# Linear attention in a two-layer decoder: the gated levels built each from the one below, and the low-rank gate product taken a round ahead

## The chip, the cores and the metric

The program runs on one core of one Trainium2 chip. A core has five engines that run side by side[...]: TensorE (PE, with its weight loads shown as PEld), VectorE (DVE), ScalarE (ACT), GpSimd (POOL) and SyncE (SP). The metric is the device time of one launch in microseconds. Three runs of the kernel before gave 1299.35, 1300.39 and 1302.56 us; the median is 1300.39.

## What is computed

The reference is a decoder of two layers over x (8 sequences of 256 tokens, width 256). Each layer has an attention, a cross-attention and a mixture of experts, and each of the six is followed by an added residual and a layer norm. The change touches the first of the six alone, the gated linear attention:

```python
q = heads(x @ Wq, DK) * scale            # 4 heads of 64
k = heads(x @ Wk, DK)
v = heads(x @ Wv, DV)                    # 4 heads of 128
gk = heads(log_sigmoid(x @ gk_w1 @ gk_w2 + gk_b2) / 16, DK)
def step(S, inp):
    S = S * exp(g_t)[..., None] + k_t[..., None] * v_t[..., None, :]
    o_t = einsum('bhk,bhkv->bhv', q_t, S)
g = x @ Wg
o = rms(o) * g_norm_w * silu(g)
x = layernorm(x + o @ Wo)
```

gk_w1 is 256x16 and gk_w2 is 16x256, so the gate comes from a product of low rank. The output at token t is a sum over s up to t of v_s, weighted by q_t, k_s and the product of the decays exp(g) of all tokens between s and t.

## The kernel before

The kernel has no recurrence. It splits the sum over pairs (s, t) by levels. At level w (1, 2, 4, ..., 128, the list WIDTHS) tokens are cut into blocks of 2w; s lies in the left half of a block, t in the right half. The decay between them is the product from the middle of the block to t, which is multiplied into q, times the product from s to the middle, which is multiplied into k. So each level has its own queries ql and keys kl, and a plain product of the two gives all its pairs. Channels lie on the 128 partitions (two groups j of 128 channels, two heads h in each), tokens along the free axis; a tile of one batch is 128 x 2 x 256.

The function gla holds the stage. Its work is a list called steps; in round b each step is called for batch b plus an offset, and the rounds run from -2 to 6, with a last part for batch 7 that is mixed with the start of the cross-attention. The order of the list is the order of work on TensorE, and the scheduler then places the instructions of the other engines. In the order of the list, with the offset:

- decays (+1): p_r, the product with w1 (L51, written through the helper mm); VectorE copies it to rt (L234); p_z, the product with w2, where rt carries a row of ones for the bias; ScalarE then takes Abs, Exp, Ln (L242 to L244), VectorE the difference e (L245), ScalarE the Exp that gives al (L246). Then the loop over levels: ql is qT times al on the right halves (L255, VectorE), kl is kT times be on the left halves (L260, POOL). tot (L267) holds the products of whole blocks; be (L271, POOL) and al (L275, VectorE) are multiplied by them on one half each to reach the next level. be is set to one and takes its first values on POOL (L250, L269).
- near (0), for chunk 0 and later for chunk 1 of 128 tokens: six small products p_near in 32x32 blocks, levels up to 16; a masked multiplication m (L310), a sum s (L315), and four copies into aT (L319), two of them on VectorE and two on POOL.
- turn (-1): transposes of the outputs of the batch before, pt_o (L374), copied to oT.
- far (0): the levels 32, 64 and, for chunk 1, 128: p_far, copied by ScalarE into aT and bT (L340 to L346).
- values and gates (+1): p_v and p_g; project (-1): p_y, residual and norm (L110 to L122).
- outputs (0): p_o from aT, bT and v; the square on ScalarE (L358), its sum ss on VectorE (L360), a power on POOL (L362), the scaled result on (L365).
- turn_in (+2): transposes of the input batch, pt_in, copied to xT (L209); turn_batch (-1): transposes of the normalised x, pt_x, copied to xT (L130).
- queries_keys (+2): p_q and p_k; qT is scaled by VectorE (L220), kT copied by ScalarE (L222).

ql and kl are kept in tiles that are set to zero once at the start, two for each level (L188), because each level writes only one half of each block and the other half has to stay zero. PSUM has one pool of eight banks that every product takes from in turn.

Of the kernel before, what the change touches and what calls it, by code (L numbers as in the profile page):

```python
# [10 lines left out]
F32 = mybir.dt.float32  # L11
BF16 = mybir.dt.bfloat16
I32 = mybir.dt.int32
AF = mybir.ActivationFunctionType
# [4 lines left out]
P = 128  # L19
# [20 lines left out]
def decoder_kernel(ctx: ExitStack, tc: tile.TileContext, a, out):  # L40
# [7 lines left out]
    def mm(dst, pairs):  # L48
        n = len(pairs)
        for i, (l, r) in enumerate(pairs):  # L50
            nc.tensor.matmul(dst, l, r, start=(i == 0), stop=(i == n - 1))  # L51
# [101 lines left out]
    def gla(late_loads):  # L153

        back = ExitStack()
        bw = back.enter_context(tc.tile_pool(name="gla_bw", bufs=1, side="right", reuse_waits="tile"))
        bk = back.enter_context(tc.tile_pool(name="gla_bk", bufs=2, side="right", reuse_waits="tile"))  # L160
# [2 lines left out]
        gp = front.enter_context(tc.tile_pool(name="gla_g", bufs=2, reuse_waits="tile"))  # L163
        wk = front.enter_context(tc.tile_pool(name="gla_wk", bufs=2, reuse_waits="tile"))

        w1 = load_k(wp, "w1", a["L0_attn_gk_w1"], 16, nc.scalar)
        w2 = wp.tile([17, 256], F32, tag="w2", name="w2")
        nc.scalar.dma_start(out=w2[0:16, :], in_=a["L0_attn_gk_w2"])
        nc.scalar.dma_start(out=w2[16:17, :], in_=a["L0_attn_gk_b2"].unsqueeze(0))
        gw = load_col(bw, "gw", a["L0_attn_g_norm_w"], nc.scalar)  # L170
        wq = load_k(wp, "wq", a["L0_attn_Wq"], 256)
        wkk = load_k(wp, "wkk", a["L0_attn_Wk"], 256)
# [18 lines left out]
            return r  # L191

        made = []
        rts = kept(wp, [17, S], "rt", 1.0)
        qls, kls = {w: [] for w in WIDTHS}, {w: [] for w in WIDTHS}
        for i in range(2):
            for w in WIDTHS:
                for n, l in (("q", qls), ("k", kls)):
                    if n == "q" or w > 1:
                        l[w] += kept(wp, [P, 2, S], f"{n}l{w}_{i}_", 0.0, 1)  # L200
        aTs = kept(bw, [P, 2, 2, P], "aT", 0.0, 4)
        qT, kT, v, gate, bT, po_, on, y = {}, {}, {}, {}, {}, {}, {}, {}

# [7 lines left out]
        def queries_keys(b):  # L211
            for name, w, d in (("q", wq, qT), ("k", wkk, kT)):
                d[b] = gp.tile([P, 2, S], F32, tag=name, name=name + "T")
                p = ps.tile([P, 2, S], F32, tag="ps", name="p_" + name)
                for j in range(2):
                    mm(p[:, j, :], [
                        (w[:, dc, j * P:(j + 1) * P], xT[:, dc, S * b:S * (b + 1)]) for dc in range(2)
                    ])
                if name == "q":
                    nc.vector.tensor_scalar(d[b], p, 0.125, None, ALU.mult)  # L220
                else:
                    nc.scalar.copy(  # L222
                        d[b].rearrange("p j t -> p (j t)"), p.rearrange("p j t -> p (j t)")
                    )

        def halves(t, w):

            return t.rearrange("p j t -> p (j t)").rearrange("p (n h w) -> p n h w", h=2, w=w)

        def decays(b):  # L230
            rt = rts[b % 2]
            p = ps.tile([P, 2, S], F32, tag="ps", name="p_r")
            mm(p[0:16, 0, :], [(w1[:, dc, :], xT[:, dc, S * b:S * (b + 1)]) for dc in range(2)])
            nc.vector.tensor_copy(rt[0:16, :], p[0:16, 0, :])  # L234
            z = ps.tile([P, 2, S], F32, tag="ps", name="p_z")
            for j in range(2):
                mm(z[:, j, :], [(w2[:, j * P:(j + 1) * P], rt)])

            e = wk.tile([P, 2, S], F32, tag="e", name="e", bufs=1)
            al = gp.tile([P, 2, S], F32, tag="al", name="al")  # L240
            flat = [t.rearrange("p j t -> p (j t)") for t in (e, z, al)]
            nc.scalar.activation(flat[0], flat[1], AF.Abs)  # L242
            nc.scalar.activation(flat[0], flat[0], AF.Exp, scale=-1.0)
            nc.scalar.activation(flat[0], flat[0], AF.Ln, bias=ones[:, 0:1])  # L244
            nc.vector.scalar_tensor_tensor(e, z, 0.0, e, ALU.min, ALU.subtract)  # L245
            nc.scalar.activation(flat[2], flat[0], AF.Exp, scale=1.0 / 16.0)  # L246


            be = gp.tile([P, 2, S], F32, tag="be", name="be")
            nc.gpsimd.memset(be, 1.0)  # L250
            tot = flat[2]
            for w in WIDTHS:
                n = 2 * S // (2 * w)
                pair = tot.rearrange("p (n h) -> p n h", h=2)
                nc.vector.tensor_tensor(  # L255
                    halves(qls[w][b % 2], w)[:, :, 1, :], halves(qT[b], w)[:, :, 1, :],
                    halves(al, w)[:, :, 1, :], ALU.mult,
                )
                if w > 1:
                    nc.gpsimd.tensor_tensor(  # L260
                        halves(kls[w][b % 2], w)[:, :, 0, :], halves(kT[b], w)[:, :, 0, :],
                        halves(be, w)[:, :, 0, :], ALU.mult,
                    )
                if w == WIDTHS[-1]:
                    break
                nxt = gp.tile([P, n], F32, tag=f"tot{w}", name=f"tot{w}")
                nc.vector.tensor_tensor(nxt, pair[:, :, 0], pair[:, :, 1], ALU.mult)  # L267
                if w == 1:
                    nc.gpsimd.tensor_copy(halves(be, 1)[:, :, 0, 0], pair[:, :, 1])  # L269
                else:  # L270
                    nc.gpsimd.tensor_tensor(  # L271
                        halves(be, w)[:, :, 0, :], halves(be, w)[:, :, 0, :],
                        pair[:, :, 1:2].broadcast_to([P, n, w]), ALU.mult,
                    )
                nc.vector.tensor_tensor(  # L275
                    halves(al, w)[:, :, 1, :], halves(al, w)[:, :, 1, :],
                    pair[:, :, 0:1].broadcast_to([P, n, w]), ALU.mult,
                )
                tot = nxt

        def values(b, c):
            if c == 0:
# [12 lines left out]
        def near(b, c):  # L295

            p = [ps.tile([P, 2, NEAR, 32], F32, tag="ps", name="p_near") for _ in range(2)]
            for l in range(NEAR):
                w = 2 ** l // 2
                k = kls[w][b % 2] if w > 1 else kT[b]  # L300
                q = qls[w][b % 2] if w else qT[b]
# [12 lines left out]
            for h in range(2):  # L314
                nc.vector.tensor_reduce(s[:, h], m[:, h].rearrange("p j l t -> p j t l"), AX.X, ALU.add)  # L315
            aT = aTs[2 * (b % 2) + c]
            for i in range(4):
                r = slice(32 * i, 32 * i + 32)
                (nc.gpsimd.tensor_copy if i % 2 else nc.vector.tensor_copy)(aT[r, :, :, r], s[r])  # L319

        def far(b, c):
# [3 lines left out]
            for w, s0, s1, t0, t1 in ((64, 0, 64, 64, 128), (32, 0, 64, 32, 64), (32, 64, 128, 96, 128)):  # L325
                for j in range(2):
                    for h in range(2):
                        r = slice(64 * h, 64 * h + 64)
                        mm(p[h][s0:s1, 0, j, t0:t1], [
                            (kls[w][b % 2][r, j, o + s0:o + s1], qls[w][b % 2][r, j, o + t0:o + t1])  # L330
                        ])
            if c:
                for j in range(2):
                    for h in range(2):
                        r = slice(64 * h, 64 * h + 64)
                        mm(p[h][:, 1, j, :], [(kls[P][b % 2][r, j, 0:P], qls[P][b % 2][r, j, P:S])])

            aT = aTs[2 * (b % 2) + c]
            for h in range(2):
# [38 lines left out]
        def project(b):  # L378
# [7 lines left out]
            (decays, 1),  # L386
            (near, 0, 0),
            (turn, -1, 0),
            (far, 0, 0),
            (values, 1, 0),  # L390
            (turn, -1, 1),
# [6 lines left out]
            (outputs, 0, 0),  # L398
            (turn_in, 2),
            (outputs, 0, 1),  # L400
            (turn_batch, -1),
            (queries_keys, 2),
        ]
        for b in range(-2, B - 1):
            run(round_of(steps, b))
# [987 lines left out]
```

## Time and profile before

| what | value |
|---|---|
| median of three runs | 1300.39 us |
| the profiled run | 1301.57 us |
| its span, first to last instruction | 1299.8 us |
| mean granted clock of TensorE | 0.888 |
| busy: PE, PEld, DVE, ACT, POOL | 1054.2, 692.1, 655.3, 448.4, 339.9 us |
| DMA, mean rate over the span | 48 GB/s |

The linear attention takes about the first 300 us of the span. The page's second part gives the busy share of each engine in tenths, in 40 slices of 32.5 us; the first nine slices are this stage:

```
PE   6888888888898649999997468888998888873870
DVE  6667676654555432222222544444444566764325
ACT  3445454424444212212121134333443444330104
POOL 7545555430111021111111730000000110101544
```

A line of a timeline has the start, the length, the engine, the line of the code, the operation, and what it writes and reads; the brackets at its end give the time that the engine sat idle before it, and what released it. A chain of waits is followed back from the last instruction of a window: at each step to what released it, or to the instruction before it on its engine. In a table of groups, the numbers at the end are the busy time of the group, the mean length of one in ns, and the idle time before them.

### The profile page before, as it was taken

To read this page: it belongs to the slowest core of one execution; us is meant where nothing else is said; L and a number is where in the kernel's file an instruction comes from. 1 tells how busy PE (TensorE), PEld (TensorE's weight loads), DVE (VectorE), ACT (ScalarE), POOL (GpSimd) and SP (SyncE) were. 2 spreads that over 40 slices of the span, in tenths; PEclk is the share of its full clock that TensorE was granted. 3 is DMA by queue.
4 is the path that set the end of the run, shared out by engine and by line. 5 is a ranking of instruction groups with operands and counts; after the bars stand their busy time and mean duration, and the time that the engine had idled before them with its cause. 6 is when DMAs were issued, how large, how long until landed. Compare 5 with 4: busy or idle time off the path is not lost.

```text
span 1299.8 us, 25292 instructions
## 1 busy us (share of the span) xinstructions
PE 1054.2 (81%) x10221; PEld 692.1 (53%) x10221; DVE 655.3 (50%) x1833; ACT 448.4 (34%) x874; POOL 339.9 (26%) x454
## 2 busy tenths in 40 slices
PE   6888888888898649999997468888998888873870
PEld 4556665665665426666665235555555555652540
DVE  6667676654555432222222544444444566764325
ACT  3445454424444212212121134333443444330104
POOL 7545555430111021111111730000000110101544
PEclk9789988889999659999999689899999998975895
DMA  7000000003111291111111210000000010105425
GB/s 191 3 2 2 3 3 2 2 3 130 34 33 34 61 303 45 49 41 49 45 45 57 77 49 2 1 1 1 2 1 1 2 33 18 34 24 150 138 82 174
DMA packets 54517, 62.64 MB, mean 48 GB/s; under 512 B 10897, under 2 KB 45858, under 8 KB 54402
## 3 DMA queue, kind: packets, MB, share of 16 engines
q1 hardware_dynamic: 46368, 44.59, 10.6%
q0 software_dynamic: 5616, 15.34, 4.2%
q8 instruction: 82, 1.34, 0.4%
q10 hardware_dynamic: 2418, 1.09, 0.4%
q14 instruction: 33, 0.27, 0.1%
HBM read 42.78 MB, written 18.22 MB: 47 GB/s over the span
## 4 chain that ended last, share of the span: by engine, by line
PE 56%; DVE 24%; ACT 5%; POOL 5%; issue 4%; DMA 4%; SPq 0%; POOLq 0%; ACTq 0%; DVEq 0%
PE p_y L51 6%; PE p_u L1013 5%; PE p_y L1035 5%; PE p_v L1013 5%; PE p_pv L51 4%; DVE m L687 3%; PE p_q L51 3%; PE p_v L51 3%; PE p_s L681 3%; PE p_st L585 2%; PE p_k L51 2%; PE p_st L696 2%; DVE tot L267 2%; DVE al L275 2%; PE p_s L51 2%
## 5 line engine op out<-in xcount | busy, mean ns | idle before, releaser
L687 DVE TENSOR_REDUCE m<-p_s 128x2 f32<-128x512 f32 x128 | 80.1, 683 | 31.8 <-PE p_s L681 31.8
L1019 DVE TENSOR_TENSOR h<-h,p_v 128x512 f32<-128x512 f32 x39 | 26.8, 688 | 121.1 <-PE p_v L1013 121.1
L896 POOL DMA_INDIRECT xg<-rows,tok x39 | 37.0, 949 | 178.3 <-PE pt_g L1002 158.9
L122 DVE TENSOR_TENSOR y<-p_y,xb 128x512 f32<-128x512 f32 x24 | 16.5, 688 | 118.0 <-PE p_y L51 118.0
L1013 PE MATMUL p_u<-fw,xgT 128*128 x156 | 75.3, 606 | 0.6 <-DVE xgT L1004 0.6
L499 POOL TENSOR_TENSOR xb<-x,L_xattnbo 128x512 f32<-128x512 f32 x16 | 20.3, 1271 | 210.6 <-DVE y L122 169.6
L703 ACT ACTIVATE e<-p_st 128x512 f32<-128x512 f32 x128 | 66.9, 643 | 22.6 <-PE p_st L468 20.2
L1035 PE MATMUL p_y<-fw,hT 128*128 x312 | 73.8, 379 | 0.7 <-ACT hT L1028 0.7
L1013 PE MATMUL p_v<-fw,xgT 128*128 x156 | 74.0, 597 | 0.0
L1035 PEld LDWEIGHTS p_y<-fw,hT 128*128 128x128 f32 x312 | 59.2, 190 | 25.2 <-issue 18.2
L592 ACT ACTIVATE e<-p_st 77x512 f32<-77x512 f32 x128 | 65.7, 600 | 17.7 <-PE p_st L468 17.7
L1028 ACT COPY hT<-pt_h 128x512 f32<-128x512 f32 x39 | 22.8, 585 | 128.7 <-PE pt_h L1026 128.7
L477 ACT COPY u<-p_pv 128x512 f32<-128x512 f32 x48 | 28.1, 585 | 110.9 <-PE p_pv L51 109.9
L51 PE MATMUL p_pv<-e,vals 77*32 77x256 f32 (+1 forms) x1024 | 64.8, 394 | 0.0
L130 ACT COPY xT<-pt_x 128x512 f32<-128x512 f32 x40 | 23.4, 585 | 111.1 <-PE pt_x L129 110.5
L499 POOL TENSOR_TENSOR xb<-x,L_attnbo 128x512 f32<-128x512 f32 x8 | 10.1, 1268 | 189.4 <-DVE y L122 189.4
L129 PE MATMUL pt_x<-ident,x 128*128 128x128 f32 x160 | 28.2, 301 | 37.9 <-DVE x L115 37.5
L576 DVE TENSOR_REDUCE m<-p_s 128x4 f32<-128x308 f32 x128 | 53.0, 467 | 6.9 <-PE p_s L51 6.9
L51 PEld LDWEIGHTS p_pv<-e,vals 77*32 77x32 f32 (+1 forms) x1024 | 33.5, 112 | 32.0 <-issue 18.2
L1013 PEld LDWEIGHTS p_v<-fw,xgT 128*128 128x128 f32 x156 | 30.1, 193 | 38.2 <-issue 38.2
L681 PE MATMUL p_s<-kT,qT 32*128 32x512 f32 x256 | 50.0, 696 | 0.0
L260 POOL TENSOR_TENSOR kl<-kT,be 128x256 f32<-128x256 f32 x56 | 48.2, 861 | 4.4
(271 smaller groups left out, 2420.1 us busy)
## 6 DMA issues: line engine op xcount, KB each, us to landing
fw<-in_L_ffn_W SPq DMA_DIRECT2D x24, 512.0 KB
rows<-x SPq DMA_DIRECT2D x32, 256.0 KB
ys<-yo SPq DMA_DIRECT2D x39, 128.0 KB
m<-in_L_ffn_w SPq DMA_DIRECT2D x16, 256.0 KB
z<-ys SPq DMA_DIRECT2D x8, 512.0 KB
x<-in_x SPq DMA_DIRECT2D x8, 256.0 KB
out<-x SPq DMA_DIRECT2D x8, 256.0 KB
b<-in_L_ffn_b ACTq DMA_DIRECT2D x8, 128.0 KB
```

Source lines behind the costliest of these rows:

```text
L51: nc.tensor.matmul(dst, l, r, start=(i == 0), stop=(i == n - 1))
L129: nc.tensor.transpose(pt[:, dc, c, :], x[:, 2 * b + c, dc * P:(dc + 1) * P], ident)
L260: nc.gpsimd.tensor_tensor(halves(kls[w][b % 2], w)[:, :, 0, :], halves(kT[b], w)[:, :, 0, :], halves(be, w)[:, :, 0, :], ALU.mult,)
L499: nc.gpsimd.tensor_tensor(xb, x[:, 2 * b:2 * b + 2, :], self.bo.unsqueeze(1).broadcast_to([P, 2, D]), ALU.add)
L576: nc.vector.tensor_reduce(st.less(b)[:, c, j, :], p, AX.X, ALU.max, negate=True)
L592: nc.scalar.activation(e[0:KV].rearrange("p i q -> p (i q)"), p[0:KV].rearrange("p i q -> p (i q)"), AF.Exp)
L681: nc.tensor.matmul(tiles[j].rearrange("p a m -> p (a m)"), st.qT[b][r, t, c * P:(c + 1) * P], kTs[b][r, t, :, :].rearrange("p a m -> p (a ...
L687: nc.vector.tensor_reduce(st.less(b)[:, c, j, 2 * t:2 * t + 2], p, AX.X, ALU.max, negate=True)
L703: nc.scalar.activation(e.rearrange("p i q -> p (i q)"), p.rearrange("p i q -> p (i q)"), AF.Exp)
L896: nc.gpsimd.indirect_dma_start(out=out, out_offset=None, in_=table, in_offset=bass.IndirectOffsetOnAxis(ap=index, axis=0),)
L1013: nc.tensor.matmul(p, xg[:, dc, :], w[:, bass.ds(e * (2 * FF) + dc * FF, FF)], start=(dc == 0), stop=(dc == 1),)
L1035: nc.tensor.matmul(y, hT[:, f * P:(f + 1) * P], w3[:, bass.ds(e * (4 * D) + f * D, D)], start=(f == 0), stop=(f == 3),)
```

## The change

Six things are done.

1. levels is a step of its own, at offset +1, and stands behind near and turn of chunk 0 and ahead of far; decays ends with the logarithm.
2. The queries of a level are made whole, 512 columns, from the queries of the level below, and the keys from the keys below (`qls[w, b], q = t, t`). The multiplier is broadcast from a small tile halves[w] of 4 columns per block of 2w: one, the decay of the left half, that of the right half, one. The queries take columns 0 and 1 (left halves unchanged, right halves times the left one's decay), the keys columns 2 and 3. The other half of a block is no longer zero; near masks it, and far reads only the halves that it needs. al and be are gone, and so are the zeroed tiles of ql and kl; the new tiles rotate in the pool. The last level makes only the 128 columns that far reads.
3. The product of low rank is a step of its own, low_rank at +2, a round ahead of decays. Its two halves of the contraction are not accumulated but go to two column tiles of 32, and the sum is taken in p_z, with w2 stacked twice. The row of ones for the bias comes from an activation with a bias column, on ScalarE.
4. qT is scaled by ScalarE.
5. queries_keys and low_rank stand ahead of turn_batch.
6. At the start ScalarE's queue has seven loads, where it had five, and three small tiles of weights are set to zero on VectorE.

```diff
-        w1 = load_k(wp, "w1", a["L0_attn_gk_w1"], 16, nc.scalar)
-        w2 = wp.tile([17, 256], F32, tag="w2", name="w2")
+        w1 = wp.tile([P, 2, 32], F32, tag="w1", name="w1")
+        w2 = wp.tile([64, 256], F32, tag="w2", name="w2")
+        one = wp.tile([64, 1], F32, tag="one", name="one")
...
+        for i in range(2):
+            nc.scalar.dma_start(out=w2[32 * i:32 * i + 16, :], in_=a["L0_attn_gk_w2"])
         nc.scalar.dma_start(out=w2[16:17, :], in_=a["L0_attn_gk_b2"].unsqueeze(0))
+        nc.scalar.dma_start(out=one[16:17, :], in_=a["c_iota"][0:1, 1:2])
...
+        halves = {w: kept(wp, [P, S // w, 4], f"halves{w}", 1.0) for w in WIDTHS[:-1]}
...
-                if name == "q":
-                    nc.vector.tensor_scalar(d[b], p, 0.125, None, ALU.mult)
+                nc.scalar.activation(
+                    d[b].rearrange("p j t -> p (j t)"), p.rearrange("p j t -> p (j t)"),
+                    AF.Copy, scale=0.125 if name == "q" else 1.0,
+                )
+
+        def low_rank(b):
+            p = ps.tile([P, 2, S], F32, tag="ps", name="p_r")
+            for dc in range(2):
+                mm(p[32 * dc:32 * dc + 32, 0, :], [(w1[:, dc, :], xT[:, dc, S * b:S * (b + 1)])])
+            rts[b] = wk.tile([64, S], F32, tag="rt", name="rt")
+            nc.scalar.activation(rts[b], p[0:64, 0, :], AF.Identity, bias=one[:, 0:1])
...
+        def levels(b):
+            e, z = ez.pop(b)
+            two = [halves[w][b % 2][:, :, 1:3] for w in WIDTHS[:-1]]
             nc.vector.scalar_tensor_tensor(e, z, 0.0, e, ALU.min, ALU.subtract)
+            nc.scalar.activation(
+                two[0], e.rearrange("p j t -> p (j t)").rearrange("p (n h) -> p n h", h=2), AF.Exp, scale=1.0 / 16.0
+            )
+            q, k = qT[b], kT[b]
+            for l, w in enumerate(WIDTHS):
+                last = w == WIDTHS[-1]
+                if 0 < l < len(two):
+                    nc.vector.tensor_tensor(
+                        two[l], *(two[l - 1][:, :, h].rearrange("p (n i) -> p n i", i=2) for h in range(2)),
+                        ALU.mult,
                     )
+                for n, old, side in (("q", q, 1), ("k", k, 0)):
+                    if w == 1 and n == "k":
+                        continue
+                    t = gp.tile([P, 2, P if last else S], F32, tag=f"{n}l{w}", name=f"{n}l{w}")
...
+                        f = halves[w // 2][b % 2][:, :, 0:2] if n == "q" else halves[w // 2][b % 2][:, :, 2:4]
+                        if last:
+                            v[1], f = v[1][:, side::2], f[:, side::2]
+                        (nc.vector if n == "q" else nc.gpsimd).tensor_tensor(
+                            v[0], v[1], f.unsqueeze(3).broadcast_to(v[0].shape), ALU.mult
+                        )
...
             (decays, 1),
             (near, 0, 0),
             (turn, -1, 0),
+            (levels, 1),
             (far, 0, 0),
...
             (outputs, 0, 1),
+            (low_rank, 2),
+            (queries_keys, 2),
             (turn_batch, -1),
-            (queries_keys, 2),
         ]
```

More of the change, by code (lines that the diff above doesn't have):

```diff
@@ L164, in gla @@
         wk = front.enter_context(tc.tile_pool(name="gla_wk", bufs=2, reuse_waits="tile"))
-        w1 = load_k(wp, "w1", a["L0_attn_gk_w1"], 16, nc.scalar)
-        w2 = wp.tile([17, 256], F32, tag="w2", name="w2")
-        nc.scalar.dma_start(out=w2[0:16, :], in_=a["L0_attn_gk_w2"])
+        w1 = wp.tile([P, 2, 32], F32, tag="w1", name="w1")
+        w2 = wp.tile([64, 256], F32, tag="w2", name="w2")
+        one = wp.tile([64, 1], F32, tag="one", name="one")
+        nc.vector.memset(w1, 0.0)
+        nc.vector.memset(w2, 0.0)
+        nc.vector.memset(one, 0.0)
+        nc.scalar.dma_start(
+            out=w1[:, :, 0:16], in_=a["L0_attn_gk_w1"].rearrange("(c p) n -> p c n", p=P)
+        )
+        for i in range(2):
+            nc.scalar.dma_start(out=w2[32 * i:32 * i + 16, :], in_=a["L0_attn_gk_w2"])
         nc.scalar.dma_start(out=w2[16:17, :], in_=a["L0_attn_gk_b2"].unsqueeze(0))
+        nc.scalar.dma_start(out=one[16:17, :], in_=a["c_iota"][0:1, 1:2])
         gw = load_col(bw, "gw", a["L0_attn_g_norm_w"], nc.scalar)
@@ L193, in gla @@
         made = []
[L194 to L200, printed above, removed]
+        halves = {w: kept(wp, [P, S // w, 4], f"halves{w}", 1.0) for w in WIDTHS[:-1]}
+        qls, kls, rts, ez = {}, {}, {}, {}
         aTs = kept(bw, [P, 2, 2, P], "aT", 0.0, 4)
@@ L218, in queries_keys @@
                     ])
-                if name == "q":
[L220 to L228, printed above, removed]
+                nc.scalar.activation(
[8 more added lines that the diff above has]
+            nc.scalar.activation(rts[b], p[0:64, 0, :], AF.Identity, bias=one[:, 0:1])
         def decays(b):
[L231 to L234, printed above, removed]
+            rt = rts.pop(b)
             z = ps.tile([P, 2, S], F32, tag="ps", name="p_z")
@@ L239, in decays @@
             e = wk.tile([P, 2, S], F32, tag="e", name="e", bufs=1)
-            al = gp.tile([P, 2, S], F32, tag="al", name="al")
-            flat = [t.rearrange("p j t -> p (j t)") for t in (e, z, al)]
+            flat = [t.rearrange("p j t -> p (j t)") for t in (e, z)]
             nc.scalar.activation(flat[0], flat[1], AF.Abs)
@@ L244, in decays @@
             nc.scalar.activation(flat[0], flat[0], AF.Ln, bias=ones[:, 0:1])
+            ez[b] = e, z
+        def levels(b):
+            e, z = ez.pop(b)
+            two = [halves[w][b % 2][:, :, 1:3] for w in WIDTHS[:-1]]
             nc.vector.scalar_tensor_tensor(e, z, 0.0, e, ALU.min, ALU.subtract)
[L246 to L262, printed above, removed]
-                    )
[L264 to L279, printed above, removed]
@@ new lines, in levels @@
+            nc.scalar.activation(
[8 more added lines that the diff above has]
+                        ALU.mult,
+                    )
+                for n, old, side in (("q", q, 1), ("k", k, 0)):
+                    if w == 1 and n == "k":
+                        continue
+                    t = gp.tile([P, 2, P if last else S], F32, tag=f"{n}l{w}", name=f"{n}l{w}")
+                    if w == 1:
+                        nc.vector.tensor_tensor(
+                            t.rearrange("p j t -> p (j t)").rearrange("p (n h) -> p n h", h=2),
+                            old.rearrange("p j t -> p (j t)").rearrange("p (n h) -> p n h", h=2), two[0], ALU.mult,
+                        )
+                    else:
+                        v = [
+                            e.rearrange("p j t -> p (j t)").rearrange("p (n h w) -> p n h w", h=2, w=w // 2)
+                            for e in (t, old)
+                        ]
+                        f = halves[w // 2][b % 2][:, :, 0:2] if n == "q" else halves[w // 2][b % 2][:, :, 2:4]
[3 more added lines that the diff above has]
+                            v[0], v[1], f.unsqueeze(3).broadcast_to(v[0].shape), ALU.mult
+                        )
+                    if n == "q":
+                        qls[w, b], q = t, t
+                    else:
+                        kls[w, b], k = t, t
@@ L299, in near @@
                 w = 2 ** l // 2
-                k = kls[w][b % 2] if w > 1 else kT[b]
-                q = qls[w][b % 2] if w else qT[b]
+                k = kls[w, b] if w > 1 else kT[b]
+                q = qls[w, b] if w else qT[b]
                 for j in range(2):
@@ L329, in far @@
                         mm(p[h][s0:s1, 0, j, t0:t1], [
-                            (kls[w][b % 2][r, j, o + s0:o + s1], qls[w][b % 2][r, j, o + t0:o + t1])
+                            (kls[w, b][r, j, o + s0:o + s1], qls[w, b][r, j, o + t0:o + t1])
                         ])
@@ L335, in far @@
                         r = slice(64 * h, 64 * h + 64)
-                        mm(p[h][:, 1, j, :], [(kls[P][b % 2][r, j, 0:P], qls[P][b % 2][r, j, P:S])])
+                        mm(p[h][:, 1, j, :], [(kls[P, b][r, j, :], qls[P, b][r, j, :])])
             aT = aTs[2 * (b % 2) + c]
```

## The prediction

> **What bounds the kernel now.** I read the clock of the core first (one core, mean 0.888), then the slices of the page (TensorE busy in 8 or 9 tenths up to 300 us, so the linear attention is the stage to ask about), then the chain of waits inside it, then the timeline engine by engine. The change touches only this stage. One round of it, from one decay product p_z to the next, shown by the chain from 168 to 205 us (start, length, what):
>
> ```profile
> 169.60 0.60 DVE qT L220
> 170.20 0.33 DVE rt L234
> ...
> 170.57 1.14 PE p_z L51 x4
> ...
> 178.15 0.64 ACT al L246
> ...
> 193.04 0.43 DVE ql L255
> ...
> 196.30 0.42 DVE x L115
> ...
> 202.16 1.13 DVE on L365 x4
> 203.29 0.60 DVE qT L220
> 203.88 0.33 DVE rt L234
> ```
>
> The loop is closed through VectorE. The gates of the next batch need p_z, p_z needs rt, rt is copied by VectorE, and VectorE reaches that copy only behind the levels, the norm and the two output chunks. From the list: p_z to the end of al 8.2 us (170.57 to 178.79), levels and near work 14.7 (to 193.47), norm 3.6 (to 197.0), two chunks of outputs with their waits for POOL's power 6.3 (to 203.3), qT and rt 0.9. Sum 33.7, the distance to p_z at 204.26. TensorE, in its timeline, waits for exactly this:
>
> ```profile
> 196.86 0.67 PE L129 MATMUL pt_x<-ident,x 128*128 128x128 f32 x4 [0.81 <-DVE x L115]
> ...
> 204.26 1.12 PE L51 MATMUL p_z<-rt,w 17*128 17x256 f32 x4 [2.30 <-DVE rt L234]
> ```
>
> At the start the same wait is larger, because rt of batch 1 stands behind all levels of batch 0:
>
> ```profile
> 35.58 2.04 PE L51 MATMUL p_z<-rt,w 17*128 17x256 f32 x4 [6.68 <-DVE rt L234]
> ```
>
> p_z starts at 13.87, 35.58, 67.62, 103.28, 136.93, 170.57, 204.26, 238.74; the last pt_x is at 265.16. So rounds last 32.0, 35.7, 33.65, 33.64, 33.69, 34.5, and the last 26.4 to pt_x.
>
> **What leaves, comes and moves.** *VectorE gives up qT and rt* (0.60 + 0.33 us per round, on the loop); ScalarE takes both, 0.6 and about 0.45 (nearest row: L446, 128x256 from PSUM, 0.47), ahead of the kT copy, where it idled 2.9 us waiting for p_k. rt is now made a round ahead, so p_z waits only for its turn on TensorE.
>
> *TensorE's order.* p_r, p_q, p_k now stand before pt_x. p_r in two column tiles instead of one accumulated pair: 0.95 before, bounds 0.5 (the tiles run together) and 0.95; I take 0.55, at most 0.4 a round. pt_x comes some 4 us later against p_o; its result is read only by the stage after, so that costs nothing, but p_z now stands behind it and behind x. p_z has the same columns and costs the same.
>
> *Levels.* Before, per batch: 8 ql, 7 al, 7 tot on VectorE; a memset, a copy, 7 kl, 6 be on POOL. After: 7 ql of 512 columns, one of 256, 6 tot; 6 kl of 512, one of 256. In elements nothing is saved: VectorE 15x256 plus 508 against 7x512+256 plus 504, POOL's products 13x256 = 3,328 against 6x512+256 = 3,328. That matters because the two engines take turns. POOL's timeline and then VectorE's at the same moment:
>
> ```profile
> 189.02 0.89 POOL L271 TENSOR_TENSOR be<-be,tot 128x256 f32<-128x256 f32 x1
> 189.99 0.73 POOL L260 TENSOR_TENSOR kl<-kT,be 128x256 f32<-128x256 f32 x1
> ```
> ```profile
> 189.02 0.41 DVE L255 TENSOR_TENSOR ql<-qT,al 128x256 f32<-128x256 f32 x1
> ...
> 190.08 0.92 DVE L275 TENSOR_TENSOR al<-al,tot 128x256 f32<-128x256 f32 x1
> ```
>
> be, starting with ql, is longer than the 0.68 it takes elsewhere; al, starting inside kl, takes 0.92 instead of 0.41 and ends 0.28 after kl does: its own pass began when POOL let go. So halving the count saves only fixed parts. Prices of POOL's products:
>
> ```profile
> L260 POOL TENSOR_TENSOR kl<-kT,be 128x256 f32<-128x256 f32 x56 | 48.2, 861 | 4.4
> ...
> L271 POOL TENSOR_TENSOR be<-be,tot 128x256 f32<-128x256 f32 x48 | 37.0, 772 | 3.8
> ```
> ```profile
> L499 POOL TENSOR_TENSOR xb<-x,L_xattnbo 128x512 f32<-128x512 f32 x2 | 2.5, 1264 | 0.1
> ```
>
> The trace has no wide kl, so bounds: 1.27 (the wide xb, 1.271 over the page, also with one operand broadcast, VectorE idle) and 1.72 (twice the 0.861). I take 1.27 and add VectorE's turns separately. The Trainium skill, "GPSIMD Engine Reference", section "Performance versus the Vector engine", speaks against leaving these on POOL: about 2.6 cycles per element for two inputs. On top of the 0.861 that makes 0.861 + 256 x 2.6 / 1.2 GHz = 1.42 each, an estimate, 0.9 us more per round than 1.27. The row has the same shape and decides; the 0.9 stays in the range.
>
> POOL from al to the last half of aT was 15.16 us (178.79 to 193.95). After: 6 x 1.27 + 0.86 = 8.5, gaps 0.6. VectorE's own passes there are about 4,344 elements at 1.0 ns ((688 - 433) / 256, rows L1019 and L255) = 4.3; 7 gaps and dispatches take in some 1.4 of them, so POOL is stretched by 2.9. Then VectorE's reduction for the second chunk must end and POOL copies aT (0.83): about 1.5 more. The sum is 13.5; in a second count over VectorE (passes 4.7, tots 1.25, m and s 2.4, waits for POOL 5.5 of its 7.5 us, then aT) it is 14.8. I take 14.3. If VectorE waited only as long as before (4.1) it would be 12.9, if for all 7.5, 16.3.
>
> *POOL's order.* Its aT copies of chunk 0 (1.17 us, amid the levels before) now stand ahead of the first kl; they wait for s, which is done 3 us before the Exp, so they cost nothing unless near is late.
>
> *The exponential comes later.* In the changed kernel's order ScalarE does six copies from p_far (1.25 us) before the Exp with its table load (1.93), and VectorE two m and two s (2.5) before e. From the end of p_z: near 3.2, m and s to 5.7, e 6.4; the far copies to 7.0; Exp to 9.0. Before it was 7.1 (171.7 to 178.79).
>
> **The new loop.** End of p_z to Exp 9.0; to aT of chunk 1, 14.3; p_o of chunk 1 behind it 1.8; p_r 0.55, p_q 1.73, p_k 1.77, pt_x 0.55 (durations start to start); p_z 1.05; handovers 0.5. That is 31.3 us against 33.65. What is late next is POOL's chain and aT, not rt. VectorE's output chunks end about 2 us into the next round, where near still runs: covered; if not, m starts that much later.
>
> **The start.** The 30 zeroed 128x512 tiles of ql and kl go (VectorE 7.3 us, POOL 7.2), replaced by small ones: worth nothing, since VectorE's first qT at 11.66 waited only on p_q, and POOL was idle from 11.6. ScalarE issues seven loads instead of five; the sixth waits for the slot of the first batch's load (landed 3.9), so the table load ends near 6.2 and xT comes at 6.8 instead of 5.64; with p_q and p_k at half rate and p_r in front, the first Exp is 0.9 late. Then VectorE: levels of batch 0 11.5 from 21.8, four casts 2.4, near work and e 3.2, Exp 1.95 = 40.9, where al began its levels at 45.0 before; 14.8, 1.8, 4.05 more bring the third p_z to 61.6, against 67.62: 6.0 gained. SP's and POOL's load queues keep their order; only slots shift.
>
> **Sum.** Start 6.0. Five rounds: before 171.1, after 5 x 31.3 plus 2 for the two rounds stretched by fetch stalls in near (2.5 and 2.15 us of "issue") = 158.5: 12.6 gained. The last round has no p_r, p_q, p_k to hide behind: 9.0 + 13.9 + norm 3.4 + handovers against 25.3 puts pt_x 1.4 later. Total 17.2. 1301.57 - 17.2 = 1284.4; the profiled run is 1.2 above the median of 1300.39, so **1283**. Nothing after 300 us changes but its start.
>
> **The clock.** The windows (start:end, length, TensorE, ...; the clock is third from the end):
>
> ```profile
> 172.00:174.00 2.00, 2.00 (x162) 1.94 (x161) 0.27 (x1) 1.97 (x3) 0.00 (x0) 0.55 0.04 8
> ...
> 180.00:182.00 2.00, 2.00 (x195) 1.83 (x193) 2.00 (x5) 0.98 (x2) 1.84 (x3) 1.00 0.03 8
> ```
>
> After the 2.3 us wait and the thin near products TensorE runs at half clock for 3 to 7 us in nearly every round: p_v at 176.79 takes 3.08 instead of 1.98. The Trainium skill, "TensorE: Matmul & The Clock Gate", section "HAM oscillation", asks for no idle gap over about 3.4 us; by that rule no gap here ever closes the gate and closing the wait wins nothing more. By the rows it closed after 2.3. I counted half of the slow time away (near 3.2, not 3.7); if all goes, near and far are 1.2 us shorter, 6 us over five rounds.
>
> **Rivals.** *TensorE becomes the bound* (0.15): if the turns cost less than before, only its own work is left: 26.5 us of products at full clock, 1.5 of fetch stalls, 1 of slow clock = 29.0 per round; 171.1 - 145 + 6 = 32, so 1268. For it: TensorE's waits are 3.4 us of 33.7. Against: the shared turns. *Only the start counts* (0.2): the later Exp and 16.3 for the levels give 33.3 per round; start 6, last round -1.4: about 1295. For it: element counts do not fall. *Slower* (0.06): the wide kl on POOL. Seven products now hang on one another, and every 0.1 us more of each of six costs 4.8 us over eight batches; from 1.27 + 17.2 / 48 = 1.63 us on, all is lost. At 1.8 (twice 0.86 to 0.99) it is 25.4 - 17.2 = 8 slower, 1308. Against: the 1.27 row. *It does not do what it says* (0.04): p_z held by another wait, no change, 1300.
>
> **Chances.** The forecast (0.55) spans 1275 to 1291. With the rivals, and 1272 to 1299 from the two bounds of the levels, I range from 1269 to 1297. 0.3% is 3.9 us, about what a measurement here can tell from no change. Faster 0.86 (forecast, TensorE, most of start-only), same 0.08, slower 0.06.
>
> **What would show it.** p_z no longer released by rt but following pt_x; the second p_z near 29 us; rounds of 31 to 32; wide kl at 1.3 to 1.6; p_o waiting for POOL's aT; Exp some 9 us behind p_z. Rounds of 29 with TensorE without waits would show the first rival, kl over 1.63 the slow one; a third p_z not before 65 us would break my start.

## The result, and the profile after

The changed kernel takes 1280.25 us (median of four runs, 1276.43 to 1281.39) against 1299.89 us before (a fourth run gave 1299.40): ratio 0.9839, 95% interval 0.982 to 0.9858, or 1.6% less. Timed again on another chip, where the kernel before took 1298.25, it was 0.9868 (0.9838 to 0.9898). The profiled execution took 1279.57 us, with a span of 1277.8 and a mean clock of 0.902; before, the span was 1299.8.

The predicted 1283 us lies close by. The parts of the prediction are another matter, and they begin with the chain of waits of the changed kernel over the round that answers to the one shown of before (start, length, what):

```profile
158.00 1.07 PE p_z L51 x4
...
166.58 0.69 ACT halves L257
...
167.99 1.64 DVE halves L264
...
179.74 0.72 DVE s L328
180.46 0.33 DVE ql L286
180.79 0.72 DVE s L328
...
181.96 0.30 POOL aT L332
182.26 0.04 issue
182.31 3.45 PE p_o L51 x16
185.75 0.56 PE p_r L51 x4
...
190.40 1.06 PE p_z L51 x4
```

rt has gone from the chain: behind p_k comes pt_x, then p_z at once. The chain now runs through the exponential (it ends at 167.27, 8.2 us behind the end of p_z and 9.3 behind its start), the levels, POOL's copy into aT (182.26, 15.0 later), and the second output chunk. TensorE's timeline at the same places, and at the second p_z of the kernel (start, length, engine, line, what, and in brackets the wait before it):

```profile
27.73 1.13 PE L51 MATMUL p_z<-rt,w 64*128 64x256 f32 x4
...
182.31 0.80 PE L51 MATMUL p_o<-v,aT 128*128 128x128 f32 x2 [2.66 <-POOL aT L332]
...
190.33 1.13 PE L51 MATMUL p_z<-rt,w 64*128 64x256 f32 x4
```

The second p_z starts at 27.73 without a wait, where it stood at 35.58 with 6.68 us of one. The new wait is 2.66 us for aT, and it is not all that it costs. The windows around it (the clock is the third number from the end):

```profile
178.00:180.00 2.00, 1.64 (x13) 1.25 (x11) 2.00 (x5) 1.36 (x3) 0.61 (x1) 1.00 0.00 0
180.00:182.00 2.00, 0.00 (x0) 0.00 (x0) 1.95 (x5) 0.31 (x1) 0.32 (x2) 0.96 0.00 0
182.00:184.00 2.00, 1.70 (x8) 1.70 (x9) 1.66 (x6) 0.00 (x0) 0.36 (x2) 0.50 0.00 0
184.00:186.00 2.00, 2.00 (x14) 1.71 (x13) 1.05 (x3) 0.21 (x1) 0.83 (x2) 0.68 0.00 0
186.00:188.00 2.00, 2.00 (x12) 1.58 (x9) 0.59 (x3) 0.82 (x2) 1.20 (x2) 1.00 0.00 0
```

In this round the half clock stands behind p_o's wait, where before it stood in the near products behind p_z's: the 16 products take 3.45 us. Not every round is like it. TensorE's lines of two other rounds, and one of e2, a run described below:

```profile
86.52 0.49 PE L51 MATMUL p_o<-v,aT 128*128 128x128 f32 x2 [0.77 <-POOL aT L332]
...
148.48 0.80 PE L51 MATMUL p_o<-v,aT 128*128 128x128 f32 x2 [2.84 <-POOL aT L332]
```
```profile
164.95 0.49 PE L51 MATMUL p_o<-v,aT 128*128 128x128 f32 x2 [2.94 <-POOL aT L322]
```

From p_z to this product it is 24.4 us in four of the five rounds that follow the third p_z, and 24.8 in the last. Behind waits of 0.77, 0.64 and 0.51 us the clock stayed full, and the next p_z followed 6.6 us later; behind 2.84 and 2.66 us it followed 9.4 and 8.0 us later. So the five rounds last 31.0, 31.0, 33.8, 32.4 and 31.4 us. The length of the wait alone does not settle the clock: in e2 it stayed at 1.00 behind 2.94 us. Over the five rounds the mean clock is 0.95, and was 0.91 before.

The levels, in the groups of the page (x48: six in each of eight batches; busy us, mean ns | idle time before, and its releaser):

```profile
L286 POOL TENSOR_TENSOR kl<-kl,halves 128x512 f32<-128x512 f32 (+1 forms) x48 | 60.0, 1249 | 20.6 <-DVE halves L264 18.9
...
L264 DVE TENSOR_TENSOR halves<-halves 128x256 f32<-128x256 f32 (+5 forms) x48 | 53.8, 1120 | 0.0
```

A total of 256 down to 8 columns takes 1.12 us on the mean. Why is seen where POOL's timeline is laid beside VectorE's:

```profile
169.80 1.57 POOL L286 TENSOR_TENSOR kl<-kl,halves 128x512 f32<-128x512 f32 x1 [0.67 <-DVE halves L264]
171.79 1.45 POOL L286 TENSOR_TENSOR kl<-kl,halves 128x512 f32<-128x512 f32 x1 [0.42 <-DVE halves L264]
...
176.72 1.06 POOL L286 TENSOR_TENSOR kl<-kl,halves 128x512 f32<-128x512 f32 x1 [0.19 <-DVE halves L264]
```
```profile
169.56 0.68 DVE L286 TENSOR_TENSOR ql<-ql,halves 128x512 f32<-128x512 f32 x1
170.16 1.46 DVE L264 TENSOR_TENSOR halves<-halves 128x128 f32<-128x128 f32 x1
```

The total begins at 170.16, while POOL is in kl, and ends at 171.62, 0.25 after kl does; the next kl then needs that total. In turn kl, begun inside ql, takes 1.57, and 1.06 where only the masking product m, which reads PSUM, was running when it began. The Trainium skill, "SBUF — State Buffer", section "SBUF: two separate sides", states the rule behind this: a GpSimd operation and a VectorE one with two SBUF inputs shut each other out for a whole instruction. Row and rule agree.

**Where the 22.0 us of the profiled execution come from.** The third p_z comes 5.5 us sooner (62.13 for 67.62); the five rounds to the eighth (221.77 for 238.74) give 11.5; the last round takes 1.1 back (pt_x of the sixth batch at 249.33 for 265.16). That is 15.8. Another 2.9 come up to the next pt_x, where batch 7 is mixed with the cross-attention: p_k and p_y, which took 2.72 and 5.69 us before (mean clock 0.66 from 276 to 286 us), take 1.50 and 3.72 (clock 1.00 from 261 to 268 us). Some 3.1 come in the last experts' stage, whose code is the same, from the first weight load to the first result fetched (77.6 before, 74.5 after). The run on the other chip had its eighth p_z at 220.41 and 74.3 for that stage.

### The profile page after: what moved, and what is told of

Its sections match the earlier page's. It is cut to its first block, busy times and chain, and to the rows that moved or that the text cites. A ratio compares the mean times of both kernels' runs of the same rounds, so it can differ in the third digit from the quotient of the medians.

```text
span 1277.8 us, 25121 instructions
## 1 busy us (share of the span) xinstructions
PE 1040.9 (81%) x10221; PEld 685.3 (54%) x10221; DVE 651.4 (51%) x1747; ACT 457.9 (36%) x890; POOL 308.8 (24%) x381
## 4 chain that ended last, share of the span: by engine, by line
PE 59%; DVE 22%; ACT 6%; POOL 4%; issue 4%; DMA 3%; SPq 1%; POOLq 0%; ACTq 0%; DVEq 0%
PE p_u L1028 5%; PE p_y L51 5%; PE p_y L1050 5%; PE p_v L1028 5%; PE p_pv L51 4%; PE p_q L51 3%; DVE halves L264 3%; DVE m L702 3%; PE p_k L51 3%; PE p_s L696 3%; DVE ql L286 3%; PE p_st L711 2%; PE p_v L51 2%; PE p_st L600 2%; PE p_s L51 2%
## 5 line engine op out<-in xcount | busy, mean ns | idle before, releaser
L702 DVE TENSOR_REDUCE m<-p_s 128x2 f32<-128x512 f32 x128 | 80.1, 684 | 32.1 <-PE p_s L696 32.1
L607 ACT ACTIVATE e<-p_st 77x512 f32<-77x512 f32 x128 | 65.8, 602 | 18.2 <-PE p_st L483 18.2
L286 POOL TENSOR_TENSOR kl<-kl,halves 128x512 f32<-128x512 f32 (+1 forms) x48 | 60.0, 1249 | 20.6 <-DVE halves L264 18.9
L130 ACT COPY xT<-pt_x 128x512 f32<-128x512 f32 x40 | 23.4, 585 | 107.7 <-PE pt_x L129 107.1
L264 DVE TENSOR_TENSOR halves<-halves 128x256 f32<-128x256 f32 (+5 forms) x48 | 53.8, 1120 | 0.0
L51 PEld LDWEIGHTS p_pv<-e,vals 77*32 77x32 f32 (+1 forms) x1024 | 33.7, 113 | 32.4 <-issue 18.4
```

What stands on the lines that cost most here:

```text
L264: nc.vector.tensor_tensor(two[l], *(two[l - 1][:, :, h].rearrange("p (n i) -> p n i", i=2) for h in range(2)), ALU.mult,)
L286: (nc.vector if n == "q" else nc.gpsimd).tensor_tensor(v[0], v[1], f.unsqueeze(3).broadcast_to(v[0].shape), ALU.mult)
L607: nc.scalar.activation(e[0:KV].rearrange("p i q -> p (i q)"), p[0:KV].rearrange("p i q -> p (i q)"), AF.Exp)
L702: nc.vector.tensor_reduce(st.less(b)[:, c, j, 2 * t:2 * t + 2], p, AX.X, ALU.max, negate=True)
```

## The experiments

The changed kernel once more and e1 to e12 (there is no e3) were timed in five rounds beside the kernel before (medians of that one: 1303.84 for the first four, 1298.25 for the next four, 1305.95 for the last). The ratio is the total's; the three p_z and the mean round (third to eighth p_z, over five) come from one profiled execution of each, and show the linear attention alone. Between the two profiles of the changed kernel the third p_z differs by 2.0 us and the mean round by 0.1.

| run | ratio, 95% interval | p_z 2, 3, 8 (us) | round |
|---|---|---|---|
| before | 1 | 35.6, 67.6, 238.7 | 34.2 |
| changed kernel | 0.9839 (0.982, 0.9858) | 27.7, 62.1, 221.8 | 31.9 |
| changed kernel again | 0.9868 (0.9838, 0.9898) | 27.8, 60.1, 220.4 | 32.1 |
| e1 loop opened only | 0.979 (0.9759, 0.9822) | 28.3, 58.0, 210.6 | 30.5 |
| e2 levels only | 1.0072 (1.0044, 1.0099) | 34.0, 68.8, 246.9 | 35.6 |
| e4 products before p_o | 0.9805 (0.9771, 0.9839) | 28.6, 56.3, 208.8 | 30.5 |
| e5 near together | 0.9883 (0.9859, 0.9908) | 28.5, 57.7, 222.4 | 32.9 |
| e6 levels early | 0.9836 (0.9815, 0.9856) | 27.8, 60.0, 215.3 | 31.1 |
| e7 e1 and e4 | 0.977 (0.9747, 0.9794) | 28.4, 56.0, 209.0 | 30.6 |
| e8 totals as logs | 0.9843 (0.9824, 0.9862) | 35.7, 63.6, 214.5 | 30.2 |
| e9 ahead, on VectorE | 0.9824 (0.9798, 0.9851) | 32.4, 64.2, 216.6 | 30.5 |
| e10 in round, on ScalarE | 0.9831 (0.9804, 0.9859) | 28.8, 59.0, 216.7 | 31.5 |
| e11 e7 and turn_in first | 0.9709 (0.968, 0.9737) | 27.6, 54.5, 203.7 | 29.9 |
| e12 whole tiles, all of it | 0.9831 (0.9803, 0.9859) | 37.6, 65.8, 218.7 | 30.6 |

**The change in two halves.** e1 takes the kernel before and opens the loop only; the levels stay in decays with al and be:

```
-            rt = rts[b % 2]
...
+            rt = rts.pop(b)
...
             (outputs, 0, 1),
+            (low_rank, 2),
+            (queries_keys, 2),
             (turn_batch, -1),
-            (queries_keys, 2),
```

> The kernel before, with only the loop opened: low-rank product a round ahead in two column tiles, rt and the scaled query copied by ScalarE, products of the batch after next ahead of pt_x; the levels stay as they were (half-filled tiles, al and be, inside the decays step). Theory A (the gain is the opened loop): the start gains its 5.5 us and a round is p_z to Exp 7.1, levels to aT 15.2, then 9.2 of p_o to p_z as measured in the changed kernel = 31.5 us, 0.9 less than the changed kernel's 32.4 in the round I read: 1275 us, anywhere in 1270 to 1282. Rival B (the whole levels bring half of the gain, by fewer turns between VectorE and POOL): 1286 to 1295.

e2 is the other half, the changed kernel with rt, the scaled query and that order put back:

> The changed kernel's levels (whole tiles, a step of their own), but the low-rank product, its copy rt and the scaled query as before: in the round itself, on VectorE, products of the batch after next behind pt_x. Theory A: the loop through VectorE stays closed, p_z to Exp 8.2, levels 15.0, norm 3.6, output chunks 6.3, qT and rt 0.9 = 34.0 us against 33.7 before, and the second p_z stays near 35: no gain, 1297 to 1307 us. Rival B: 1286 to 1293.

e1 took 1278.68 us, ratio 0.979: at least the whole gain. e2 took 1314.55, slower than before by 0.7% (0.4 to 1.0%). Theory A holds, and more than it said: the half named "levels" costs time. In e2 the loop is the old one, list by list: from p_z's start to the Exp's end 9.5 us (175.55 to 185.02), to aT 15.0, norm and chunks 9.7, copies 0.9, in sum 35.1. The 34.0 expected had left out p_z's own 1.05.

In e1 ScalarE turns to the Exp after one copy of oT, not after it and six copies from p_far, and in the round shown the last aT is there when TensorE comes. ScalarE's, POOL's and TensorE's timelines of e1, for the round from 149.53 to 179.59:

```profile
157.10 0.63 ACT L257 ACTIVATE al<-e 128x512 f32<-128x512 f32 x1
...
172.02 0.83 POOL L330 COPY aT<-s 32x128 f32<-32x128 f32 x2
...
172.63 0.60 PE L217 MATMUL pt_in<-ident,x 128*128 128x128 f32 x4
173.07 0.39 PE L51 MATMUL p_o<-v,aT 128*128 128x128 f32 x2
173.29 0.39 PE L51 MATMUL p_o<-v,bT 128*128 128x128 f32 x2
```

From Exp to aT it is 15.1 us (157.73 to 172.85) with the old levels and 15.0 with the new: the whole tiles gave nothing there. The Exp ends 8.2 us after p_z starts, not 9.3. In the two of e1's five rounds in which p_o waits for aT it follows p_z by 23.4 us, not 24.4; these waits, 1.4 and 1.9 us, left the clock full, and the next p_z follows p_o by at most 6.6 us in every round. e1 keeps the tiles that are set to zero at the start, and its second p_z comes only 0.6 us later than the changed kernel's: dropping them was worth next to nothing, as predicted.

**Which half of the opening.** Both start from e1. e9 puts rt and the scaled query back on VectorE and keeps the low-rank product ahead; e10 keeps ScalarE and puts the product back directly before p_z, and the queries and keys behind pt_x (main lines of each edit against e1):

```
-            nc.scalar.activation(rts[b], p[0:64, 0, :], AF.Identity, bias=one[:, 0:1])
+            nc.vector.tensor_scalar(rts[b], p[0:64, 0, :], one[:, 0:1], None, ALU.add)
```
```
+            (low_rank, 1),
             (decays, 1),
...
-            (low_rank, 2),
-            (queries_keys, 2),
             (turn_batch, -1),
+            (queries_keys, 2),
```

> The opened loop with the old levels, but rt and the scaled query copied by VectorE as in the kernel before: only the place of the low-rank product (ahead of pt_x, for the batch after next) is changed. In VectorE's order rt then stands behind the first output chunk, not behind both, and at the start behind most of batch 0's levels. Theory J (the distance opens the loop; the engine matters at the start only): second p_z near 33 us instead of 28.3, rounds of 30.3 to 31, eighth p_z at 215 to 220, ratio to the kernel before 0.983 to 0.988. Rival K (it is the move to ScalarE that opens it): p_z waits 2 us or more for rt in each round, rounds of 32.5 to 33.5, eighth p_z at 226 to 234, ratio 0.992 to 0.999.

> The opened loop with the old levels, but the low-rank product in the round itself again, directly ahead of p_z and behind pt_x, its copy on ScalarE. Theory L (either half opens the loop: on ScalarE rt waits for one copy only): p_z waits some 1.0 to 1.5 us for rt in every round, rounds of 31.0 to 31.8, eighth p_z at 215 to 219, ratio 0.982 to 0.987. Rival M (the distance is needed): rounds of 32.5 and more, eighth p_z beyond 224.

TensorE's timelines of e9 (second and third p_z) and e10 (second and sixth):

```profile
32.44 1.60 PE L51 MATMUL p_z<-rt,w 64*128 64x256 f32 x4 [4.04 <-DVE rt L240]
...
64.16 1.13 PE L51 MATMUL p_z<-rt,w 64*128 64x256 f32 x4
```
```profile
28.84 1.13 PE L51 MATMUL p_z<-rt,w 64*128 64x256 f32 x4 [0.57 <-ACT rt L238]
...
153.50 1.13 PE L51 MATMUL p_z<-rt,w 64*128 64x256 f32 x4 [0.57 <-ACT rt L238]
```

Theories J and L hold: distance opens the rounds (30.5 with rt on VectorE), the engine opens the start (VectorE's rt is 4 us late there, behind batch 0's levels), and a rt on ScalarE in the round costs 0.57 us of waiting, less than the 1.0 to 1.5 expected. e10's mean round is 1.0 longer than e1's: between p_o and p_z stand now the 0.57 for rt and some 0.8 us in which pt_x, ahead of p_q and p_k again, waits for x (3.3 us in four waits from 62 to 210 us). e9's ratio, 0.9824, lies just below the 0.983 to 0.988 of theory J; its places in the stage are those expected.

**Undoing what the levels cost.** e6 calls levels directly behind decays. e8 keeps the step and makes the totals as sums of logarithms:

```
-            (levels, 1),
...
             (decays, 1),
+            (levels, 1),
```
```
+                    nc.vector.tensor_tensor(
+                        t, *(g[:, :, h].rearrange("p (n i) -> p n i", i=2) for h in range(2)), ALU.add
+                    )
+                    g = t
+                nc.scalar.activation(two[l], g, AF.Exp, scale=1.0 / 16.0)
```

> The changed kernel itself, as the measure for the runs beside it on the same chip. In its first profile the eighth p_z started at 221.8 us and the last product of the experts' second network stage began about 3 us sooner after its start than in the kernel before, for no reason in the code. Both theories: 1278 to 1285 us, eighth p_z within 1.5 us of 221.8.

> The changed kernel with its levels called right after the decays again, ahead of the near products, instead of behind the first turn: whole tiles kept, the step of its own undone. Theory E (what the changed kernel loses to the opened loop with the old levels is the exponential, which stands behind six copies): the Exp ends 8.2 us after p_z starts instead of 9.3, TensorE reaches p_o when aT is ready, rounds of 30.0 to 30.5, eighth p_z at 211 to 213 us, total 1273 to 1279. Rival F (the whole tiles themselves are slower, because each small total waits for POOL's wide product): rounds of 31.5 to 32.5, eighth p_z at 218 to 222, total as the changed kernel.

> The changed kernel with the totals of each level made as sums of the logarithms on VectorE and one Exp of each on ScalarE (six more Exps of 256 to 8 columns), so that no small product on VectorE stands between two of POOL's wide ones. Theory G (the shared turns set the 15.0 us from Exp to aT: 48 totals took 53.8 us, 6.7 a batch, nearly all of it waiting): Exp to aT 12 to 13, p_o no longer waits, rounds of 30 to 30.5, eighth p_z at 210 to 213. Rival H (the sums wait for POOL in the same way, since they too are products of two operands in VectorE's queue, and only their place changes): rounds of 31.5 to 32.5, eighth p_z at 218 to 223.

The control had its eighth p_z where expected. In e6 the Exp ends 8.2 us after p_z starts (159.65 for 151.40), but the mean round is 31.1, between theory E and rival F, and the total is not told apart from the control's. Of the 1.5 us per round by which the changed kernel stands behind e1, the step of its own is some 0.9. The other 0.5 cannot be put down to the whole tiles: four of e6's five rounds are 30.5 us on the mean, where the same four of e1 are 30.4, and the fifth took 33.1, with p_v and p_y at half clock (3.35 and 5.41 us, elsewhere 1.98 and 3.72) and no wait of p_o. In e8 POOL has no wait between wide products any more:

```profile
163.29 1.75 POOL L287 TENSOR_TENSOR kl<-kT,halves 128x512 f32<-128x512 f32 x1 [3.33 <-ACT halves L265]
165.12 9.03 POOL L287 TENSOR_TENSOR kl<-kl,halves 128x512 f32<-128x512 f32 x6
175.60 0.61 POOL L333 COPY aT<-s 32x128 f32<-32x128 f32 x2 [1.45 <-DVE s L329]
```

From Exp (163.16) to aT (176.21) it is 13.05, p_o does not wait in this round, and the rounds are 30.2: theory G, on the steady rounds. H had a point too, since four of the sums still stood 1.05 to 1.32 us each. And the start gave it back: on ScalarE the gates of batch 0 and the copy of the next input stand among the totals' Exps, which wait for VectorE's sums, with two more table loads of 1.28. So the second p_z came at 35.73, and the total equals the changed kernel's.

**Filling the wait.** e4 puts TensorE's next products where it waited; e5 puts both chunks' near products together, ahead of the levels:

```
+            (low_rank, 2),
+            (queries_keys, 2),
             (outputs, 0, 1),
-            (low_rank, 2),
-            (queries_keys, 2),
```
```
             (near, 0, 0),
+            (near, 0, 1),
...
-            (near, 0, 1),
             (values, 1, 1),
```

> The changed kernel with the low-rank product and the products for queries and keys put ahead of the second output chunk, so that TensorE has 4.2 us of work where it waited 2.7 for POOL's last copy into aT. Theory A (that wait and the half clock behind it are on the loop): per round 2.7 of waiting and some 1.6 of p_o at half clock go, until TensorE's own 29 us bind: 3 us in each of six rounds, 1262 us, 1257 to 1268. Rival C (POOL's and VectorE's chain binds the round whatever stands in front of p_o, and ScalarE's three copies now delay the square of the second chunk): 1276 to 1284.

> The changed kernel with both chunks' near products one after the other, ahead of the levels, so that VectorE masks and sums the second chunk before the levels begin, and aT of that chunk no longer stands behind them. Theory A (aT behind the levels closes the loop): p_o never waits for aT, TensorE's 29 us bind: 1260 to 1268. Rival D (the 3 us of mask and sum only move ahead of e and the Exp, so the levels end 3 us later, and the next round's near products wait for the last ql or kl): 1276 to 1290.

In e4 the wait is gone, the third p_z comes 5.8 us sooner than in the changed kernel and the rounds are 30.5: half of the 3 us expected. TensorE then waits only for the copy of xT, 0.7 us a round, but from 60 to 220 us it also idles 13.6 us for which the trace shows no wait; with these its own work fills 30.5 us, not 29. The total, 1279.37, lies in the rival's numbers. The profiled execution is 1.2 us longer than the changed kernel's though its eighth p_z comes 12.9 sooner: of these 14 us, 5 came back in the second layer's attention (347.7 us for 342.8, with a clock of 0.90 for 0.92) and 3 in the last experts' stage (77.6 for 74.5), whose code is the same. e5 missed: its total, 1289.30, lies in rival D's range, but not for D's reason. p_o never waits in it, but the waits of the changed kernel and of e5 from 60 to 220 us (total, times, longest) show what took its place:

```profile
PE p_near L51 <- issue: 7.6, 5, 2.2
PE p_o L51 <- POOL aT L332: 7.4, 5, 2.8
```
```profile
PE p_near L51 <- issue: 20.1, 10, 2.3
```

"issue" is idle time for which the profile shows no wait. The near products of two chunks in a row stall twice a round, for 2 us each; apart they stall once. The 12.5 us more of it, less the 7.4 of p_o's waits, are the 1.0 us by which each of the five rounds is longer than the changed kernel's. What the stall is, no run here shows.

**Towards the best version.** e7 is e1 with e4's order; e11 also puts turn_in ahead of the first output chunk; e12 gives the whole tiles every help at once:

```
+            (turn_in, 2),
             (outputs, 0, 0),
-            (turn_in, 2),
```

> The opened loop with the old levels, and the low-rank, query and key products ahead of the second output chunk. If TensorE's own work binds the opened loop's rounds of 30.0 us already (it waited twice for aT there, 3.3 us over five rounds), this gains at most 0.6 us a round: eighth p_z at 207 to 211 us, total within 4 us of the opened loop alone. If p_o's wait for aT is still on the loop, rounds of 28.5 and an eighth p_z at 201 to 205.

> The opened loop with the old levels and the products ahead of the second output chunk, and besides the transposes of the input of the batch after next ahead of the first output chunk, so that the low-rank product doesn't wait for their copy (0.7 us in each of five rounds). If TensorE's order is the bound: rounds shorter by 0.7, eighth p_z at 203 to 206 us, ratio 0.972 to 0.976. If aT or the levels bind, the same as without it: 208 to 210, ratio 0.977.

> The changed kernel's whole tiles with everything that the runs pointed to: levels directly behind the decays, totals as sums of logarithms, products ahead of the second output chunk, transposes of the input ahead of the first. If TensorE binds both this and the run with the old levels, rounds are equal, 28.5 to 29.5, and only the start differs (second p_z near 35, as with the log totals before, since the gates' Silu stands between the totals' Exps there): eighth p_z at 206 to 211, ratio 0.976 to 0.980. If the wide products on POOL still bind: rounds of 30 to 30.5, eighth p_z at 212 to 216, ratio 0.981 to 0.985.

e7 came as expected: eighth p_z at 209.0, and a ratio of 0.977 where e1, on another chip, had 0.979. In e11 the wait of p_r is gone, the round is 29.9, the eighth p_z is at 203.7, and it took 1267.65 us where the kernel before took 1305.95: 0.9709 (0.968 to 0.9737), just below the 0.972 expected, and ahead of the changed kernel in both of its timings. The levels of before with the loop opened are the better kernel among these; the whole tiles with plain totals were not run with all the moves at once. e12 missed: a second p_z at 37.59 and rounds of 30.6, so that the eighth comes at 218.7. Its trace has single waits of TensorE for VectorE's m and sum (2.8 and 2.2 us), and what binds it was not settled.

## Why the prediction was right, and where it was not

- *The loop through VectorE, opened by the rt a round ahead*: shown. e1 alone brings the gain, e2 without it none, and e9 and e10 tell which half does what.
- *The start, 6.0*: 5.5 (the run again: 7.5). The first Exp was not 0.9 late but 0.7 early (it ended at 20.13, before at 20.81), and the second ended at 38.9, not 40.9. Then the second output chunk of batch 0 waited 4.6 us for aT, and it ran at half clock, 3.7 us where the sum had 1.8.
- *Five rounds, 12.6*: 11.5. From p_z to p_o the sum has 1.05 + 9.0 + 14.3 = 24.35 us, and 24.4 was measured, but two errors cancel in it. The Exp ended 8.2 us after the end of p_z, not 9.0: the near products, put at 3.2, took 1.8 at full clock, and the copies from p_far behind them ended at 6.2, not 7.0. The levels took 15.0, not 14.3: POOL's seven products with their turns ended at 179.19, 11.9 us after the Exp (12.0 in the first count), but the sums of the second chunk and aT behind them took 3.1, not the 1.5 of that count; the count over VectorE, 14.8, was the better one. Its 5.5 us of waits for POOL is borne out by the totals alone: 53.8 / 8 = 6.7 us a batch, less the 1.25 taken for their own passes.
- *p_o at 1.8*: the mis-sized term. Behind p_o the sum has 6.9 us up to the next p_z. At full clock 6.6 were measured, with p_o at 2.0, in three of the five rounds; in the other two p_o took 3.7 and 3.4, and the whole stretch 2.8 and 1.4 more. The prediction named the wait for aT as what is late next, but gave p_o no half clock behind it. That half of the slow time would vanish is borne out by the mean clock (0.91 before, 0.95 after). The rule that it set beside its rows (no idle gap over some 3.4 us: the Trainium skill, "TensorE: Matmul & The Clock Gate", section "HAM oscillation") does not tell these rounds apart: the clock was 0.50 after 2.66 us and 1.00 after 2.94 in e2.
- *The 2 us for stalls in near*: not what made two rounds longer. The stalls (7.6 us from 60 to 220) stand ahead of p_o, which waits for aT after them, and p_z to p_o stays at 24.4 us. They happen to stand in the sum for the 4.2 us of half clock that it lacked; that the five rounds agree within 1.1 us is in part luck.
- *The wide kl at 1.27*: 1.06 undisturbed, 1.74 where VectorE's ql and total stand beside it, 1.43 on the mean of 48. The 1.42 estimated from the Trainium skill, "GPSIMD Engine Reference", section "Performance versus the Vector engine", was too high for the product alone. The mean stayed below the 1.63 at which the slow rival would have taken over.
- *The last round, 1.4 lost*: 1.1.
- *The step of its own*: priced at 1.9 us a round against 0.9 won by the whole tiles. The sum held this, and the text did not draw the consequence, that the opened loop with the old levels would be faster. The runs give some 0.9 for the step, and for the tiles nothing won: 15.0 us from Exp to aT with them, 15.1 without.
- *TensorE as the bound, 29.0*: not in the changed kernel. It is near in e11, at 29.9, and e11 is 1268 us, the number of that rival, though this agreement of totals is partly chance: that chip was slower by 6 us.
- *Only the start counts*: by its own numbers (33.3 per round, 6.0 and -1.4) that rival comes to 1291 to 1293, not about 1295.
- The total was met in part by luck: no term held the 2.9 us of clock at the change of stages, nor the 3.1 in a stage whose code is the same. The terms that it held gave 15.8 of the 17.2 us.

## What to carry to other kernels

A value that closes a loop through a busy engine is worth producing one round earlier, or on an engine that is idle at that moment; look for the one copy that stands last in a long queue before rewriting the work in front of it. A change of several parts should be measured in its parts: here one gained 2%, the others cost up to 0.7%, and the whole looked like a success. When an added wait is priced, look at the clock of the products behind it as well (here 1.4 and 2.8 us more behind waits of 2.7 and 2.8, nothing more behind 0.8), and look whether TensorE has later work that could stand in front.

## What was not expected of the hardware

The same code at the end of the kernel, from the first weight load of the last experts' stage to the first fetch of its results, took 74.2 to 81.6 us in these profiles (77.6 before, 74.5 after, 81.6 in e1, 80.4 in e11). The windows of the changed kernel and of e1 there, six us each, show where the time went:

```profile
1198.10:1204.10 6.00, 5.87 (x28) 4.41 (x27) 2.61 (x7) 1.28 (x3) 4.70 (x5) 1.00 0.39 112
```
```profile
1189.48:1195.48 6.00, 1.89 (x6) 1.27 (x6) 1.93 (x5) 1.05 (x2) 3.31 (x4) 0.83 0.17 48
1195.48:1201.48 6.00, 6.00 (x18) 4.28 (x18) 1.18 (x3) 1.05 (x2) 1.57 (x3) 0.60 0.23 64
```

Thirty us into the stage TensorE of e1 stands idle for some 4 us and then has a clock of 0.60, where the changed kernel goes on at 1.00. Why it stood still there was not followed up. A span that differs by 5 us thus proves little about a change in another stage; the places inside the stage do.
